# Layer 3 gather loop: offset convolution and indices two blocks ahead, the next image's transform in 17 turns of four per block

## The chip, the cores and the metric

The kernel runs on one core of a Trainium2 chip. The metric is the device time of one execution in microseconds (us). Other times are taken from one profiled execution.

## What is computed

Four layers run one after the other on a batch of four images of 96 channels and 64 x 64 pixels. The change lies in the fourth one (layer 3). For an image it computes, cut to what matters here:

```python
mag  = abs(rfft2(x))                       # -> channel gate ca; with x -> spatial gate sa
y    = x * ca * sa
freq = resize(abs(rfft2(y)).mean(1))
aux  = concat([y, coord, freq])            # 101 channels
offset = conv3x3(aux, off_w)               # 9 taps x 2 coordinates
gate   = sigmoid(conv1x1(relu(conv3x3(aux, dg1_w)), dg2_w))
y_base = conv3x3(y, base_w)
sampled = bilinear(y, xx + offset_x, yy + offset_y)    # 9 taps, 4 corners each
y_def = einsum("bcthw,oct->bohw", sampled, def_w)
z = (1 - gate) * y_base + gate * y_def     # then batch norm, relu, + x
```

## The kernel before

An image's 4096 pixels are cut into 8 blocks (m) of 512, and each block into 4 steps (u) of 128 pixels: 32 blocks and 128 steps in the loop for the four images. The order on every engine is the one in which the program writes it down (a manual schedule), so a waiting instruction holds up all that stands behind it on its engine. The parts of a step and of a block, with their engines:

- gathered(u) (L1970): nine indirect DMAs on GpSimd (L1976), one per tap; each fetches for 128 pixels the four corners of all channels from a table in DRAM. They need the indices ix of the block and a free sm buffer; there are three, so gathered(u) reuses the one that weighted(u-3) read.
- weighted(u) (L1983): ten VectorE operations (L1993 to L1997) multiply sm by the corner weights cw, which lie in PSUM, and add them up into sd.
- transposed(u) (L1999): seven TensorE transposes of sd (L2014), copied by ACT into sT (L2015, L2017).
- mixed(m) (L2019): seven matmuls on sT (yd, L2026); then four VectorE operations beginning with z (L2031), which need yd and write the block's result.
- guides(m) (L1907): the offset and gate convolution (go, nine taps on TensorE, L1899) and two ACT operations (L1912, L1913).
- offsets(m) (L1915): four transposes (of, L1920), then 16 small VectorE operations from L1927 to L1956 that make the indices ix (L1950) and the weights cw of the block.
- bases(m) (L1959): the base convolution (yb, nine taps), a matmul dg, and two ACT operations (L1964, L1968).

While an image is in the loop, the next one is prepared, in chains of four half steps each; every step has two such places, "early" (ahead of weighted) and "late" (behind it):

- attended(b, n), eight per image (L1842): the transfer sab of the spatial gate (L1849, SyncE) and the multiplication of X by both gates (L1851, VectorE); four transposes tp (L1576); the ACT copy xT (L1581) and eight writes of it into the table (L1858, SyncE); four matmuls fa with ACT copies (L1592, L1600).
- columns(b, f0), nine per image (L1864): transposes tf (L1612); an ACT copy fT (L1619); matmuls fb (L1623) and their square on ACT; an addition on VectorE (L1629).
- frequency(b) (L1880): a root on ACT, 33 matmuls fe (L1640) and a copy, one matmul up, and two DMAs that write the frequency channel, which guides of the next image read.

In the loop, gathered(u) is written first, then the early places, then weighted(u-1) and transposed(u-1), then the late ones. Relative to the four steps of block k: mixed(k-1) stands at the second step (matmuls early, z late), guides(k+1) at the second step early, offsets(k+1) at the third (transposes early, VectorE late), bases(k+1) at the fourth early. The chains of attended begin at half steps 1, 5, 9, ... of the 64 of an image, two to a block; columns follow from step 17 on, one each step; frequency takes steps 27 and 28. Before the loop a front (L2047) transforms all images, applies the gates to the first, and makes the first block's guides, offsets and bases.

Of the kernel before, what the change touches and what calls it, by code (L numbers as in the profile page):

```python
# [10 lines left out]
F32 = mybir.dt.float32  # L11
I32 = mybir.dt.int32
# [1783 lines left out]
def layer3(k, X, aux, out):  # L1796

    tc, nc, ins = k.tc, k.nc, k.ins
    with ExitStack() as es:
# [42 lines left out]
        def attended(b, n, tags=None):  # L1842

            table = tables[b % 2]
            s = slice(n * NB, n * NB + NB)
            if n == 0:
                f1[b] = spec.begin()
            sab = wk.tile([C, NB], F32, name="sab")
            nc.sync.dma_start(sab, sa_d[b : b + 1, s].partition_broadcast(C))  # L1849
            y = X[b][:, s]  # L1850
            nc.vector.scalar_tensor_tensor(y, y, ca[:, b : b + 1], sab, ALU.mult, ALU.mult)  # L1851
            yield
            for yT in spec.row_steps(f1[b], 4 * n, y, None, tags):
                if yT is not None:
                    for h2 in range(2):
                        for q in range(4):
                            r, c = 8 * n + h2 + 1 - q // 2, 1 - q % 2
                            nc.sync.dma_start(  # L1858
                                table[r : r + 7 : 2, c : c + W, q].rearrange("r w c -> w r c"),
                                yT[64 * h2 : 64 * h2 + 64],  # L1860
                            )
                yield

        def columns(b, f0, tags=None):  # L1864

            yield from spec.column_steps(f1[b], f0, tags)
# [40 lines left out]
        def guides(m):  # L1907

            p = ps.tile([128, NB], F32, name="go_ps", tag="cv")
            conv(m, p, go_w, 101)  # L1910
            go[m] = wk.tile([82, NB], F32, name="go")
            nc.scalar.activation(go[m][64:82], p[64:82], AF.Identity, bias=go_b[64:82])  # L1912
            nc.scalar.activation(go[m][:50], p[:50], AF.Relu, bias=go_b[:50])  # L1913

        def offsets(m):  # L1915

            n = m % NN
            p = ps.tile([128, NJ, 18], F32, name="of_ps", tag="stp", bufs=1)
            for j in range(NJ):
                nc.tensor.transpose(  # L1920
                    p[:, j], go[m][64:82, 128 * j : 128 * j + 128], k.ident[64:82, 64:82]
                )
            yield
            pt = wk.tile([128, 2, 36], F32, name="pt3")
            pv = p.rearrange("p j (t a) -> p a j t", a=2)
            ptv = pt.rearrange("p a (j t) -> p a j t", t=9)
            nc.vector.tensor_scalar(ptv[:, 0], pv[:, 0], xx, None, ALU.add)  # L1927
            nc.vector.tensor_tensor(
                ptv[:, 1],
                pv[:, 1],  # L1930
                yy[:, 4 * n : 4 * n + 4].unsqueeze(2).to_broadcast([128, 4, 9]),
                ALU.add,
            )

            nc.vector.tensor_scalar(pt, pt, -1.0, float(W), ALU.max, ALU.min)
            it = wk.tile([128, 2, 36], I32, name="it")
            nc.vector.tensor_copy(it, pt)
            fl = wk.tile([128, 2, 36], F32, name="fl")
            nc.vector.tensor_copy(fl, it)
            up1 = wk.tile([128, 2, 36], F32, name="up1")  # L1940
            nc.vector.tensor_tensor(up1, fl, pt, ALU.is_gt)
            nc.vector.tensor_sub(fl, fl, up1)
            nc.vector.tensor_sub(pt, pt, fl)
            at = wk.tile([128, 36], F32, name="at")
            nc.vector.tensor_scalar(
                at, fl[:, 1], float(TW), float(TW + 1), ALU.mult, ALU.add
            )
            nc.vector.tensor_add(at, at, fl[:, 0])
            ix[m] = wk.tile([128, 36], I32, name="ix")
            nc.vector.tensor_copy(ix[m], at)  # L1950

            om = wk.tile([128, 2, 36], F32, name="om")
            nc.vector.tensor_scalar(om, pt, -1.0, 1.0, ALU.mult, ALU.add)  # L1953
            cw[m] = cws[:, m % 2]
            for i, (wy, wx) in enumerate(((om, om), (om, pt), (pt, om), (pt, pt))):
                nc.vector.tensor_mul(cw[m][:, :, i], wx[:, 0], wy[:, 1])  # L1956
            yield
# [78 lines left out]
            nc.vector.bn_stats(stats[:, b, n], z)  # L2036
            yield

        cws = ps.tile([128, 2, 36, 4], F32, name="cws", bufs=1)
        FS = list(range(0, NF, 4))  # L2040

        def once(step):

            step(0)
            yield

        def front(pool):  # L2047

            slots = {}

            def start(at, count, gen):
                for i in range(count):
                    slots.setdefault(at + i, []).append(gen)

            def chains(kind, b, ats):
                for n, at in enumerate(ats):
                    tags = pairs[at % 2]
                    if kind == "rows":
                        start(at, 3, described(b, n, pool, tags))
                    elif kind == "attended":  # L2060
                        start(at, 4, attended(b, n, tags))
                    else:
                        start(at, 4, columns(b, FS[n], tags))

            chains("rows", 0, range(0, 8))
            chains("rows", 1, [8, 9, 10, 12, 14, 16, 18, 20])
            chains("columns", 0, [11, 13, 15, 17, 19, 21, 22, 23, 24])
            chains("columns", 1, range(25, 34))
            start(29, 9, attention(0))
            chains("rows", 2, range(34, 42))  # L2070
            start(39, 9, attention(1))
            chains("attended", 0, range(42, 57, 2))
            chains("columns", 2, [45, 47, 49, 51, 53, 55, 57, 58, 59])
            chains("rows", 3, [43, 61, 63, 65, 67, 69, 71, 73])
            chains("columns", 0, range(60, 77, 2))
            start(63, 9, attention(2))
            chains("columns", 3, range(77, 86))
            start(80, 4, frequency(0))
            start(86, 1, once(guides))
            start(87, 2, offsets(0))  # L2080
            start(89, 1, once(bases))
            start(89, 9, attention(3))
            for t in sorted(slots):
                for step in slots[t]:
                    next(step)
# [4 lines left out]
        def at(where, u, step):  # L2090
            where.setdefault(u, []).append(lambda: next(step))

        def spread(h, n, step):
            for i in range(h, h + n):
                at((early, late)[i % 2], i // 2, step)

        with tc.manual_schedule():
            with tc.tile_pool(name="l3t", bufs=2) as pool:
                front(pool)
            smp = es2.enter_context(tc.tile_pool(name="l3s", bufs=3))  # L2100
            prod = ps.tile([128, 5, 2, C], F32, name="prod", bufs=1)
            for m in range(B * NN):
                u = NJ * (m + 1)
                step = mixed(m)
                at(early, u + 1, step)
                at(late, u + 1, step)
            for m in range(1, B * NN):
                u = NJ * (m - 1)
                early.setdefault(u + 1, []).append(lambda m=m: guides(m))
                step = offsets(m)  # L2110
                at(early, u + 2, step)
                at(late, u + 2, step)
                early.setdefault(u + 3, []).append(lambda m=m: bases(m))
            for b in range(1, B):
                u = NN * NJ * (b - 1)
                for n in range(NN):
                    spread(2 * (u + 2 * n) + 1, 4, attended(b, n))
                u += 2 * NN + 1
                for i, f0 in enumerate(FS):
                    spread(2 * (u + i), 4, columns(b, f0))  # L2120
                spread(2 * (u + len(FS) + 1), 4, frequency(b))
            for u in range(U + 2):
                if u == U - NN * NJ + 1:
                    x0 = spec.begin().rearrange("c f i h -> c (f i h)")[:, :L]
                    nc.sync.dma_start(x0, x_d[0])
                if u < U:
                    gathered(u)
                for step in early.get(u, ()):
                    step()
                if 1 <= u <= U:  # L2130
                    weighted(u - 1)
                    transposed(u - 1)
                for step in late.get(u, ()):
                    step()
# [46 lines left out]
```

## Time and profile before

| what | value |
|---|---|
| median of 21 runs | 8522.75 us (8498.27 to 8545.22) |
| the profiled execution | 8535.59 us; its span 8533.8 us |
| busy share over the span | TensorE 68%, VectorE 68%, ACT 45%, GpSimd 55% |
| loop of layer 3, first gather | 6407.3 us |
| first gathers of blocks 8, 16, 24, 31 | 6917.9, 7448.2, 7962.1, 8409.4 us |
| 6407 to 8409.5 us, busy | TensorE 1156, VectorE 1147, ACT 285, GpSimd 1064 us |
| mean granted TensorE clock | 0.77 |

A line of the page's groups reads: source line, engine, operation, what it writes and reads, shape, count; then the busy time in us and the mean time of one in ns; then the idle time of the engine just before these instructions and what ended most of it. "Remote" means that the profile shows no releaser, "issue" that it shows no wait. A line of a timeline reads: start and duration in us, engine, line, operation, and in brackets the idle time before it with its releaser. The ends of TensorE's matmuls are modelled.

### The profile page before, as it was taken

The page shows a single profiled execution, that of the slowest core. Times are in us where ns is not written, and L with a number is a line of the kernel's source. Part 1 is how long each engine was busy: PE and PEld are TensorE (multiplying, and loading weights), DVE is VectorE, ACT ScalarE, POOL GpSimd, SP SyncE. Part 2 cuts the span into 40 slices and gives each one's busy share as a digit, 9 for nine tenths or more (in the row PEclk, how much of TensorE's full clock was granted, in tenths as well). Part 3 has the DMA queues.
Part 4 walks back from the last instruction along what each step waited for, and adds up shares of the span by engine and source line. Part 5 has one row for each costly group of instructions (what it writes and reads, how often), then busy time and mean ns, then how long its engine had stood idle before and what let it go on. Part 6 is the DMA issues. An engine that isn't in the chain of part 4 may idle for free.

```text
span 8533.8 us, 75977 instructions
## 1 busy us (share of the span) xinstructions
PE 5800.3 (68%) x23706; PEld 2743.9 (32%) x23706; DVE 5837.1 (68%) x8303; ACT 3861.0 (45%) x7432; POOL 4693.3 (55%) x2915
## 2 busy tenths in 40 slices
PE   5667676777677676566697989798755656566553
PEld 1222222222222221422264645455443323333221
DVE  4899899988988989488753635445346556565555
ACT  4666666666666665333254645454431111111111
POOL 4787788777877887144443433324005545455553
PEclk8888878888888787787787878787876777677676
DMA  3222222222222222423210101010015444353333
GB/s 111 95 95 94 94 95 100 97 102 102 94 94 95 94 96 92 150 74 89 70 24 1 39 1 39 1 34 6 23 37 142 124 117 138 100 148 114 113 116 124
DMA packets 424411, 720.27 MB, mean 84 GB/s; under 512 B 188150, under 2 KB 190254, under 8 KB 419763
## 3 DMA queue, kind: packets, MB, share of 16 engines
q1 hardware_dynamic: 348710, 480.74, 18.1%
q0 software_dynamic: 73968, 227.47, 9.2%
q10 hardware_dynamic: 1328, 7.20, 0.2%
q8 instruction: 190, 3.11, 0.1%
q14 instruction: 215, 1.75, 0.1%
HBM read 567.04 MB, written 97.82 MB: 78 GB/s over the span
## 4 chain that ended last, share of the span: by engine, by line
PE 29%; DVE 23%; issue 15%; POOL 14%; another core or an unknown queue 8%; ACT 7%; DMA 2%; SPq 1%; DVEq 0%; POOLq 0%; ACTq 0%
POOL bt L602 7%; DVE bt L593 6%; PE mm_ps L448 6%; DVE bt L566 4%; PE sc_ps L1061 2%; PE pT_ps L1110 2%; POOL sz L526 2%; POOL w L507 2%; PE o_ps L1130 2%; DVE prod L1993 2%; DVE sm L1994 1%; PE yb_ps L1899 1%; ACT a_ps L577 1%; PE m_ps L1510 1%
## 5 line engine op out<-in xcount | busy, mean ns | idle before, releaser
L602 POOL TENSOR_TENSOR bt<-bt,Cb 128x1536 f32<-128x1536 f32 x512 | 1763.6, 3445 | 650.4 <-issue 488.3
L593 DVE TENSOR_TENSOR_SCAN bt<-a_ps,carry,bt 128x512 f32<-128x512 f32 x1536 | 1886.6, 1267 | 58.5 <-ACT a_ps L577 12.3
L1976 POOL DMA_INDIRECT sm<-table,ix x1152 | 1098.2, 953 | 1295.8 <-DVE om L1953 482.3
L577 ACT ACTIVATE a_ps<-dR,w_l_A_log 128x512 f32<-128x512 f32 x1536 | 1052.8, 685 | 535.4 <-DVE bt L593 531.1
L566 DVE TENSOR_TENSOR bt<-xR,Bb 128x1536 f32<-128x1536 f32 x512 | 885.6, 1730 | 219.7 <-issue 198.4
L448 PE MATMUL mm_ps<-h,Wk 96*128 96x512 f32 x1024 | 598.9, 751 | 272.0 <-issue 269.9
L2014 PE MATMUL sT_ps<-ident,sd 128*128 128x128 f32 (+1 forms) x896 | 223.1, 373 | 711.0 <-ACT sT L2015 431.4
L559 PE MATMUL Bb<-dbl,w_c_seln 128*128 128x512 f32 x512 | 366.6, 805 | 335.4 <-DVE bt L566 335.4
L613 PE MATMUL yp<-bt,w_c_red 128*32 128x512 f32 x3072 | 571.2, 658 | 13.2 <-POOL bt L602 13.2
L1098 POOL TENSOR_TENSOR p<-p,rs 128x392 f32<-128x392 f32 x384 | 312.0, 840 | 462.6 <-DVE rs L1096 360.7
L448 PEld LDWEIGHTS mm_ps<-h,Wk 96*128 96x128 f32 x1024 | 240.8, 242 | 636.8 <-issue 629.4
L469 PE MATMUL mm_ps<-xc,w_l_xp 96*128 96x512 f32 x256 | 218.4, 1006 | 289.5 <-POOL xc L463 289.5
L319 PE MATMUL bc_ps<-xs,w_l_bc 96*128 96x512 f32 x384 | 241.7, 762 | 215.3 <-DVE q L906 215.3
L2014 PEld LDWEIGHTS sT_ps<-ident,sd 128*128 128x128 f32 (+1 forms) x896 | 133.0, 181 | 785.0 <-ACT sT L2015 457.7
L1085 ACT ACTIVATE p<-p,rs 128x196 f32<-128x196 f32 x768 | 342.6, 449 | 84.9 <-DVE rs L1075 84.5
L2015 ACT COPY sT<-sT_ps 128x512 f32<-128x512 f32 (+1 forms) x256 | 122.1, 477 | 516.5 <-PE sT_ps L2014 265.1
L1912 ACT ACTIVATE go<-go_ps,w_l_go_b 18x512 f32<-18x512 f32 x32 | 21.7, 678 | 715.6 <-remote 557.2
L2031 DVE SCALAR_TENSOR_TENSOR z<-yd_ps,vec,yb 96x512 f32<-96x512 f32 x32 | 23.9, 747 | 463.9 <-remote 260.1
L1899 PE MATMUL yb_ps<-X,w_l_base_w 96*128 96x504 f32 (+3 forms) x576 | 313.0, 708 | 0.3 <-ACT go L1913 0.3
L1118 DVE COPY pT<-pT_ps 98x512 f32<-98x512 f32 x256 | 176.5, 690 | 172.5 <-PE pT_ps L1110 165.5
L559 PEld LDWEIGHTS Bb<-dbl,w_c_seln 128*128 128x128 f32 x512 | 118.9, 258 | 541.4 <-issue 506.6
L1993 DVE TENSOR_TENSOR prod<-sm,cws 128x960 f32<-128x960 f32 (+1 forms) x256 | 270.8, 1058 | 7.3 <-DVE cws L1956 0.4
(367 smaller groups left out, 12923.9 us busy)
## 6 DMA issues: line engine op xcount, KB each, us to landing
dR<-spread SPq DMA_DIRECT2D x384, 256.0 KB
xR<-spread SPq DMA_DIRECT2D x384, 256.0 KB
Cb<-out_states SPq DMA_DIRECT2D x256, 256.0 KB
spread<-w SPq DMA_DIRECT2D x128, 192.0 KB
spread<-dx SPq DMA_DIRECT2D x128, 192.0 KB
table<-xT SPq DMA_DIRECT2D x256, 96.0 KB
own<-vd SPq DMA_DIRECT2D x512, 36.8 KB
toep<-l_toep SPq DMA_DIRECT2D x12, 1536.0 KB
```

The costliest lines, as they stand in the source:

```text
L448: nc.tensor.matmul(p, Wk[:, i, t, hf], h[:, t : t + T], start=t == 0, stop=t == 3)
L559: nc.tensor.matmul(Bb, seln[:, nq], st["dbl"], start=True, stop=True)
L566: nc.vector.tensor_mul(bt, st["xR", hf], Bb.unsqueeze(1).to_broadcast([128, NG, T]))
L577: nc.scalar.activation(dec[n], st["dR", hf][:, q], AF.Exp, scale=A[:, i, nq, hf, q : q + 1])
L593: nc.vector.tensor_tensor_scan(t, dec.pop(n), t, carry_of(v)[:, q : q + 1], ALU.mult, ALU.add)
L602: nc.gpsimd.tensor_mul(bt, bt, st["Cb"][nq].unsqueeze(1).to_broadcast([128, NG, T]))
L613: nc.tensor.matmul(st["yp", hf][32 * q : 32 * q + 32], red, bt[:, q], start=nq == 0, stop=nq == NQ - 1,)
L1085: nc.scalar.activation(ps[n][:, h, i], ps[n][:, h, i], AF.Exp, scale=-1.0, bias=rs[n][:, 0, h, i : i + 1], accum_out=rs[n][:, 1, h, i : i ...
L1899: nc.tensor.matmul(dv[:, r0:r1, c0:c1], w_[:, t], av[b][:ch, 8 * n + r0 + dy : 8 * n + r1 + dy, c0 + dx : c1 + dx], start=t == 4, stop=t == 8,
L1976: nc.gpsimd.indirect_dma_start(sm[u][:, t].rearrange("p q c -> p (q c)"), None, samples[m // NN % 2], bass.IndirectOffsetOnAxis(ap=ix[m][: ...
L1993: nc.vector.tensor_mul(p, v[:, :, 2:4], w_[:, :, 2:4])
L2014: nc.tensor.transpose(p[: e - 128 * q, q - q0], sf[:, 128 * q : e], k.ident)
```

## The change

The offset convolution and the index arithmetic of a block are moved one block earlier: while block k is in the loop, guides(k+2) and offsets(k+2) stand where guides(k+1) and offsets(k+1) stood; bases stays. For this ix has three buffers instead of two and cws three slots instead of two, and the front makes the guides and offsets of block 1 as well. The chains of the next image's transform begin at other places: in each block of eight half steps there are four turns, at 0, 2, 5 and 7; eight chains of attended begin one half step ahead of turns 1 to 8, nine of columns at turns 10 to 18, and frequency four half steps behind the last.

```diff
-            ix[m] = wk.tile([128, 36], I32, name="ix")
+            ix[m] = wk.tile([128, 36], I32, name="ix", bufs=3)
...
-            cw[m] = cws[:, m % 2]
+            cw[m] = cws[:, m % 3]
...
-        cws = ps.tile([128, 2, 36, 4], F32, name="cws", bufs=1)
+        cws = ps.tile([128, 3, 36, 4], F32, name="cws", bufs=1)
...
-            start(86, 1, once(guides))
+            start(86, 1, once(guides, 0))
             start(87, 2, offsets(0))
-            start(89, 1, once(bases))
+            start(89, 1, once(bases, 0))
+            start(90, 1, once(guides, 1))
+            start(91, 2, offsets(1))
             start(89, 9, attention(3))
...
             for m in range(1, B * NN):
                 u = NJ * (m - 1)
-                early.setdefault(u + 1, []).append(lambda m=m: guides(m))
-                step = offsets(m)
-                at(early, u + 2, step)
-                at(late, u + 2, step)
+                if m + 1 < B * NN:
+                    early.setdefault(u + 1, []).append(lambda m=m + 1: guides(m))
+                    step = offsets(m + 1)
+                    at(early, u + 2, step)
+                    at(late, u + 2, step)
                 early.setdefault(u + 3, []).append(lambda m=m: bases(m))
             for b in range(1, B):
-                u = NN * NJ * (b - 1)
+                h = 2 * NN * NJ * (b - 1)
+                turns = [h + 2 * NJ * k + x for k in range(5) for x in (0, 2, 5, 7)]
                 for n in range(NN):
-                    spread(2 * (u + 2 * n) + 1, 4, attended(b, n))
-                u += 2 * NN + 1
-                for i, f0 in enumerate(FS):
-                    spread(2 * (u + i), 4, columns(b, f0))
-                spread(2 * (u + len(FS) + 1), 4, frequency(b))
+                    spread(turns[n + 1] - 1, 4, attended(b, n))
+                for f0, turn in zip(FS, turns[NN + 2 :]):
+                    spread(turn, 4, columns(b, f0))
+                spread(turn + 4, 4, frequency(b))
```

More of the change, by code (lines that the diff above doesn't have):

```diff
@@ L2037, in mixed, with once @@
             yield
-        cws = ps.tile([128, 2, 36, 4], F32, name="cws", bufs=1)
+        cws = ps.tile([128, 3, 36, 4], F32, name="cws", bufs=1)
         FS = list(range(0, NF, 4))
-        def once(step):
-            step(0)
+        def once(step, m):
+            step(m)
             yield
```

## The prediction

> **What bounds the kernel now.** I read the page first, then the order of the instructions on each engine in both programs, then the timeline of single blocks. Only the layer 3 loop changes: it runs from the first gather at 6407.3 us to the end of the last block at about 8500 us, of a span of 8533.8 us. The first gathers of blocks 0, 8, 16, 24 and 31 start at 6407.3, 6917.9, 7448.2, 7962.1 and 8409.4 us: 510.6, 530.3 and 513.9 us for eight blocks each with a transform of the next image in them, 447.3 us for seven blocks without one (63.9 each). From the page's groups:
>
> ```profile
> L1976 POOL DMA_INDIRECT sm<-table,ix x1152 | 1098.2, 953 | 1295.8 <-DVE om L1953 482.3
> L1912 ACT ACTIVATE go<-go_ps,w_l_go_b 18x512 f32<-18x512 f32 x32 | 21.7, 678 | 715.6 <-remote 557.2
> L2031 DVE SCALAR_TENSOR_TENSOR z<-yd_ps,vec,yb 96x512 f32<-96x512 f32 x32 | 23.9, 747 | 463.9 <-remote 260.1
> ```
>
> GpSimd waits 482.3 us for the indices: this is the wait that the change attacks. But VectorE waits 463.9 us at z, with no releaser named. One plain block, timelines of GpSimd, TensorE and VectorE (start, duration, what; idle before):
>
> ```profile
> 8133.77 0.95 POOL L1976 DMA_INDIRECT sm<-table,ix  x1 [0.30 <-issue]
> 8153.76 0.95 POOL L1976 DMA_INDIRECT sm<-table,ix  x1 [19.04 <-DVE om L1953]
> ```
>
> ```profile
> 8108.53 8.15 PE L2026 MATMUL yd_ps<-sT,w_l_def_w 128*128 128x512 f32 x14
> 8116.52 7.81 PE L1899 MATMUL go_ps<-X,w_l_go_w 101*128 101x512 f32 x18
> 8124.17 0.60 PE L2014 MATMUL sT_ps<-ident,sd 128*128 128x128 f32 x4
> ```
>
> ```profile
> 8114.10 0.55 DVE L1997 TENSOR_TENSOR sd<-sm,prod 128x384 f32<-128x384 f32 x1
> 8140.38 0.75 DVE L2031 SCALAR_TENSOR_TENSOR z<-yd_ps,vec,yb 96x512 f32<-96x512 f32 x1 [25.73 <-remote]
> ```
>
> z needs yd, which by the trace ends at 8116.7; z starts 23.7 us later, at 8140.38, which is 5.7 us after the last gather of the run was issued (8134.7). In blocks 23 to 30 this distance is 5.7 us each time. Over the loop, TensorE's results reach ACT or VectorE over 1 us late only when gathers were running (all 18 late z, all 20 late go). A run of gathers up to some 14 us old shows no lateness, one over 19 us old mostly does, and a pause of GpSimd ends it about 5 us after the last issue. So the chain of a plain block is: 36 gathers (44.8 us), 5.7 us, z (2.9), W (8.0), the indices (2.6), next gather: 64 us. (W(u) is the ten VectorE operations of weighted(u).)
>
> In blocks with the transform a second wait stands in VectorE's queue, at the multiplication of attended (L1851). Timelines of SyncE, ACT and VectorE:
>
> ```profile
> 7584.21 5.25 SPq L1858 DMA_DIRECT2D table<-xT  x8
> 7589.57 0.72 SPq L1849 DMA_DIRECT2D sab<-sa_d  x1
> ```
>
> ```profile
> 7583.70 0.49 ACT L1581 COPY xT<-tp_ps 128x384 f32<-128x384 f32 x1
> ```
>
> ```profile
> 7594.83 0.75 DVE L1851 SCALAR_TENSOR_TENSOR X<-X,ca,sab 96x512 f32<-96x512 f32 x1 [5.25 <-DMA sab<-sa_d]
> ```
>
> The sab transfer is queued on SyncE behind the eight table writes of the turn before, which wait for that turn's xT. From the start of xT to the next multiplication: 11.1 us.
>
> **The change, part by part.** Nothing is removed; the third ix and cws buffers cost no instruction.
>
> *Indices a block earlier.* VectorE's order keeps its places (z, W, indices, W, W, W); only the indices are those of a block later. The gather's wait on them goes. What is late next is its buffer: three sm buffers, so gather(u) waits for W(u-3), and the first gather of a block for the W that follows z. That W ended 2.6 us before the old start. TensorE's lateness remains, because GpSimd pauses no earlier. The second gather step waits for the W behind the indices: 3.5 + 8.0 = 11.5 us against 11.26 us for nine gathers (1.2517 each), +0.3. New plain block: 44.8 + 0.3 + 5.7 + 2.9 + 8.0 = 61.6 us, gain 2.3. Over the last image 7 x -2.3 = **-16**.
>
> Here a rule of the Trainium skill speaks against my reading: *SBUF — State Buffer*, section "Who interferes with whom", says that DMA never contends with a compute engine and that PE and ACT wait on no one. By it z would follow yd, and the block would be GpSimd's 45.1 us: 31 x (64.6 - 45.1) = 604 us saved, an estimate (64.6 is the mean of the 31 blocks to 8409.4). The rows above (23.7 us late, only beside gathers) disagree, and I go by them.
>
> *Front.* guides(1) and offsets(1) come before the loop. go (7.5 us, row at 6376.91) stands ahead of fe, which waited until 6399.52 for ACT; TensorE was free from 6394.5, so fe starts at 6402.0: +2.5, and of 0.4 ahead of up. The first gather waits for this chain (ACT maps): **+3**. The 3.5 us of indices on VectorE lie before W(0), which gathers need only 34 us later: nothing, as the first gathers cover it.
>
> *Seventeen turns.* Before, an image's eight attended turns lay two to a block over four blocks, the nine columns one to a step after them, the frequency map in the last steps. Now attended takes four places a block, over two blocks and the edge of a third. Same instructions, same DMAs (64 table writes, 8 sab); SyncE's order becomes sab, tables, sab, tables, sab, sab, tables, tables: of each four multiplications one has its sab ahead of the tables, three wait for tables of a turn just before. VectorE's order puts each in front of a different W: a stall there now delays the W that frees a gather's buffer. With E the end of a run of gathers, t the end of the W after z:
>
> - First block: z at E+5.7. ACT then does go twice, the sT copies, xT (go at 7165.30 to xT at 7168.57: 3.3 us): xT at E+9.1, multiplication at E+20.2, 0.75, W 8.0: next block's first gather at E+29. Block 45.1 + 29 = 74.1.
> - Second: xT stands on ACT behind yb, which follows TensorE's convolution: 11.6 us after t (8151.2 to 8162.8), then g: xT at t+13.4, multiplication t+24.5, W to t+33.2. The next has its sab: W to t+42. The third's tables wait for xT behind sT copies (2.2) and two fa (3.0): t+47.2, multiplication t+58.3, W to t+67.1. z, then xT at t+69.3, multiplication t+80.4, W to **t+89.2**.
> - Third: as before to t+33.2, W to t+42 and t+50; its gathers then run from t+33.2 to t+67. yd falls at about t+52, 19 us into that run. Prompt gives 67, late 67 + 5.7 + 2.9 + 8 = 83.6. The plain block's first lateness is at 18.8 us, so I take 83.6.
>
> - Columns fill two blocks. Their adds (L1629) now follow sT by some 3.5 us instead of standing behind a convolution (idle 6.5, 14.9, 0.9, 6.6 in block 20). Without late signals 55 us, with them 65.5; the nearest rows, old column blocks, are 60.6 to 63.3. I take 60 each.
> - Frequency: fe stands in the late stretch, beside z's own wait; when that cover is gone, it costs its 7 to 10 us. 64.
> - Two plain blocks, 61.6 each. Here something is won: the last three blocks of an image took 208, 215 and 214 us, because the frequency map came at the edge (ACT's copy of fe idle before it 37 us, z 39 us), now three blocks before.
>
> Per image 74.1 + 89.2 + 83.6 + 120 + 64 + 123.2 = 554.1, against 510.6, 530.3, 513.9: +43.5, +23.8, +40.2. **Sum**: 43.5 + 23.8 + 40.2 + 3 - 16 = **+94.5 us**. Against the profiled execution's 8535.6 us (span 8533.8) that is 8630; that one ran 12.9 us over the median of 21 runs, 8522.75, so I forecast 8522.75 + 94.5 = **8617 us**.
>
> **Rivals.**
> 1. *The crowded transform stays hidden.* If xT and sab are always out before VectorE comes to the multiplication (its idle there at most 5.6 us as now), each block is as a plain one, 61.6: 492.8 an image, -17.8 - 37.5 - 21.1 - 16 + 3 = -89, **8433**. For it: SyncE is nearly idle, and a multiplication waits for no work of its own block. Against: tables and sab are one in-order queue, and 11.1 us is longer than the 8.0 of one W. It decides at 31.5 us an image: if the three crowded blocks together take under 215 us (72 each, not 82), the kernel is not slower.
> 2. *Crowding is about paid* by the edge and by column blocks at 55: 3 x (2 x 5) and third blocks at 75 give 8617 - 30 - 26 = 8561, with shorter stalls 8500 to 8560.
> 3. *Longer runs of gathers.* Without the index wait GpSimd may run through five steps; then go is late and the indices hold VectorE: 45.1 + 5 + 2.5 + 3.5 + 8 = 64 a plain block, 65.5 a column block, no gain anywhere: +16 + 3 x (5 + 11) = 64 more, **8680**. For it: go is late at 25 us of a run in every block.
> That the change does nothing is excluded: the orders show the indices a block earlier and all turns moved.
>
> **How the numbers follow.** Forecast 0.60 (+40 to +150), rival 1 0.17, rival 2 0.18 (half of it within 0.2%, 0.02 faster, 0.07 slower), rival 3 0.05. 0.2% (17 us) is about what a measurement of this kernel can tell from no change. Faster 0.19, same 0.09, slower 0.72. The range reaches into rival 1, to 8465, and to 8690 for rival 3 and late signals in columns; about 0.2 is left out. The likeliest case alone: 8563 to 8673.
>
> **What would show it.** GpSimd's idle before L1976 named "DVE om" goes, and "DVE sd" or "DVE sm" (W) takes its place; VectorE's idle before L1851 grows from 119 us in the loop to over 200; blocks 1, 9 and 17 take over 80 us; plain blocks about 61.6; the last two blocks of each image lose their 10 to 15 us. I am wrong if the crowded blocks take under 72 us, or if plain blocks fall to 50 because the lateness goes.

## The result

The changed kernel is slower: 8683.1 us median (8668.3 to 8704.8, 8 runs) against 8522.7 us (8490.2 to 8553.7, 56 runs), a ratio of 1.0192 with a 95% interval of 1.0177 to 1.0207. That is +160 us where +94.5 was forecast, and 66 us above the predicted 8617: inside the whole range (8465 to 8690), 10 us above the +40 to +150 of the forecast case.

The profiled execution took 8642.6 us, 40 us under the median of its kernel (that of the kernel before was 13 us over its own). From the page of the changed kernel:

```profile
span 8640.9 us, 75992 instructions
...
L1976 POOL DMA_INDIRECT sm<-table,ix x1152 | 1099.1, 954 | 1393.2 <-DVE sd L1997 432.2
...
L1912 ACT ACTIVATE go<-go_ps,w_l_go_b 18x512 f32<-18x512 f32 x32 | 21.7, 678 | 730.9 <-remote 586.5
```

GpSimd's wait named "DVE om" (the indices) is gone. In its place stand 432 us for sd, the end of a W, which frees the buffer of a gather, and 264 us under the name "DVE pt L1928". These too are waits for the buffer, as the edge behind plain block 15 shows on VectorE and GpSimd. The gather starts 0.3 us after the end of W and before the indices behind that W are written.

```profile
7490.92 0.55 DVE L1997 TENSOR_TENSOR sd<-sm,prod 128x384 f32<-128x384 f32 x1
...
7493.61 0.33 DVE L1950 CAST ix<-at 128x36 int32<-128x36 f32 x1
```

```profile
7491.74 0.94 POOL L1976 DMA_INDIRECT sm<-table,ix  x1 [16.69 <-DVE pt L1928]
```

VectorE's groups over the whole span, two lines of the kernel before first, then three of the changed one:

```profile
L1851 DVE SCALAR_TENSOR_TENSOR X<-X,ca,sab 96x512 f32<-96x512 f32 x32 | 23.9, 747 | 180.1 <-DMA sab<-sa_d 148.2 <-issue 32.0
...
L1927 DVE TENSOR_SCALAR pt<-of_ps,w_c_xx 128x36 f32<-128x36 f32 x32 | 8.0, 251 | 95.3 <-PE of_ps L1920 95.3
```

```profile
L2031 DVE SCALAR_TENSOR_TENSOR z<-yd_ps,vec,yb 96x512 f32<-96x512 f32 x32 | 23.8, 745 | 327.8 <-remote 253.6 <-PE yd_ps L2026 74.1
...
L1851 DVE SCALAR_TENSOR_TENSOR X<-X,ca,sab 96x512 f32<-96x512 f32 x32 | 23.9, 746 | 317.1 <-DMA sab<-sa_d 295.3 <-issue 21.7
...
L1927 DVE TENSOR_SCALAR pt<-of_ps,w_c_xx 128x36 f32<-128x36 f32 x32 | 8.0, 250 | 217.8 <-PE of_ps L1920 217.8
```

VectorE waits less at z (464 us before; the share named "remote" hardly falls, from 260.1 to 253.6, and what falls is the wait for yd itself, from 157.9 to 74.1), more at the multiplication of attended (317 against 180; in the loop alone 255.9 against 119.0), and more at the indices (218 against 95). The last was not in the forecast.

Where the +107 us between the two profiled executions lie, from the first gather of each block:

| stretch | before, us | after, us | difference | forecast |
|---|---|---|---|---|
| up to the first gather | 6407.3 | 6395.1 | -12.2 | +3 |
| image 0 | 510.6 | 547.8 | +37.2 | +43.5 |
| image 1 | 530.3 | 548.8 | +18.5 | +23.8 |
| image 2 | 513.9 | 547.4 | +33.5 | +40.2 |
| image 3, seven blocks | 447.3 | 459.7 | +12.4 | -16 |
| from the last block's first gather | 124.4 | 142.1 | +17.7 | 0 |

The first three blocks of an image (forecast 74.1, 89.2, 83.6) took 72.2, 86.8, 81.7, then 72.0, 88.1, 82.1, then 72.1, 88.3, 81.9 us. Here is why the second is the longest: SyncE, VectorE and GpSimd in block 17 of the changed kernel (timelines: start, duration, what, idle before).

```profile
7578.51 5.25 SPq L1858 DMA_DIRECT2D table<-xT  x8
7583.86 1.02 SPq L1849 DMA_DIRECT2D sab<-sa_d  x2
```

```profile
7587.18 0.75 DVE L1851 SCALAR_TENSOR_TENSOR X<-X,ca,sab 96x512 f32<-96x512 f32 x1 [20.13 <-DMA sab<-sa_d]
```

```profile
7573.86 0.95 POOL L1976 DMA_INDIRECT sm<-table,ix  x1 [0.31 <-issue]
7596.03 1.21 POOL L1976 DMA_INDIRECT sm<-table,ix  x1 [21.22 <-DVE sd L1997]
```

The sab transfer is issued when the eight table writes ahead of it are out of SyncE's queue. VectorE stands 20 us at the multiplication with W behind it, and the gathers stand 21 us behind that W. (In this execution the multiplications that waited came 9.0 to 11.7 us after the xT before them, where the prediction had 11.1.)

From block 22 to 30 the loop is in another state: 65.2 to 68.7 us a block in place of 60 to 62. GpSimd, TensorE and ACT in the last image:

```profile
8115.11 0.95 POOL L1976 DMA_INDIRECT sm<-table,ix  x1 [0.30 <-issue]
8136.51 0.95 POOL L1976 DMA_INDIRECT sm<-table,ix  x1 [20.44 <-DVE sd L1997]
```

```profile
8087.77 7.81 PE L1899 MATMUL go_ps<-X,w_l_go_w 101*128 101x512 f32 x18
```

```profile
8121.42 0.68 ACT L1912 ACTIVATE go<-go_ps,w_l_go_b 18x512 f32<-18x512 f32 x1 [40.11 <-remote]
```

And VectorE there:

```profile
8124.80 0.25 DVE L1927 TENSOR_SCALAR pt<-of_ps,w_c_xx 128x36 f32<-128x36 f32 x1 [24.82 <-PE of_ps L1920]
```

The gathers no longer stop at the edge of a block. A run is still four steps long (36 gathers), but it goes from the second step of a block through the edge to the end of the first step of the next; the last run has seven steps. go, complete at 8095.6 by the trace, reaches ACT at 8121.42, 5.4 us after the run has ended. The indices stand in VectorE's queue ahead of the next W and hold it for 24.8 us. This is the wait of the prediction's rival 3, with runs of four steps where it had spoken of five, in nine of 31 blocks.

### The profile page after: what moved, and what is told of

Its sections match the earlier page's. It is cut to its first block, busy times and chain, and to the rows that moved or that the text cites. A ratio compares the mean times of both kernels' runs of the same rounds, so it can differ in the third digit from the quotient of the medians.

```text
span 8640.9 us, 75992 instructions
## 1 busy us (share of the span) xinstructions
PE 5769.1 (67%) x23706; PEld 2725.7 (32%) x23706; DVE 5839.6 (68%) x8303; ACT 3860.7 (45%) x7432; POOL 4694.5 (54%) x2915
## 4 chain that ended last, share of the span: by engine, by line
PE 29%; DVE 23%; POOL 15%; issue 14%; another core or an unknown queue 8%; ACT 7%; DMA 2%; SPq 1%; DVEq 0%; POOLq 0%; ACTq 0%
POOL bt L602 7%; DVE bt L593 6%; PE mm_ps L448 5%; DVE bt L566 4%; PE sc_ps L1061 2%; PE yb_ps L1899 2%; PE pT_ps L1110 2%; POOL sz L526 2%; DVE prod L1993 2%; POOL w L507 2%; DVE sm L1994 2%; PE o_ps L1130 2%; ACT a_ps L577 1%; DVE prod L1995 1%
## 5 line engine op out<-in xcount | busy, mean ns | idle before, releaser
L1085 ACT ACTIVATE p<-p,rs 128x196 f32<-128x196 f32 x768 | 342.6, 449 | 84.0 <-DVE rs L1075 83.6
L559 PEld LDWEIGHTS Bb<-dbl,w_c_seln 128*128 128x128 f32 x512 | 119.0, 258 | 541.2 <-issue 506.1
L1994 DVE TENSOR_TENSOR sm<-sm,cws 128x960 f32<-128x960 f32 (+1 forms) x256 | 267.8, 1046 | 0.0
```

The costliest lines, as they stand in the source:

```text
L559: nc.tensor.matmul(Bb, seln[:, nq], st["dbl"], start=True, stop=True)
L1994: nc.vector.tensor_mul(v[:, :, 0:2], v[:, :, 0:2], w_[:, :, 0:2])
```

## The experiments

Theory 1: the crowding of attended (sab behind the table writes) is the loss. Theory 2: the indices two blocks ahead cost by themselves, through longer runs of gathers. The runs were on four chips (numbers 7, 3, 1 and 15), on all of which the kernel before takes 7942 to 7947 us, not 8523. The chip of the first runs is not named in their records, and may be one of these at another time; I call it the first chip. Each kernel below is compared with the kernel before on its own chip. The kernel before has a profile on chip 3 alone, so sums that set another chip's profile beside it go across chips. The times in us that the first expectations name were meant for the first chip; on the others the ratios are what can be compared, against 1.0192 there.

**The turns alone.** The 17 turns of the diff on the kernel before; guides, offsets, ix and cws untouched.

> The kernel before with the 17 turns alone; guides and offsets stay one block ahead, ix and cws keep two buffers. Theory 1 (crowding): the three crowded blocks still take 72, 88 and 82 us, and the indices ahead had gained 2.3 us in each plain block, so this kernel is as slow as the changed one or slower, 8680 us or more. Theory 2 (the longer runs of gathers cost): without the indices ahead GpSimd pauses at each block's edge, no block is in the state of 65.7 us, plain blocks are at 64 again, and the kernel takes 8600 to 8640 us.

Measured: 8178.7 against 7944.7 us, 1.0291 (1.0262 to 1.0319), chip 7. The stall at L1851 in the loop is 260.3 us, and the crowded blocks take 48 to 56, 87 to 90 and 64 to 66 us: without the indices ahead the loss is all there, as theory 1 had it.

**Sab one chain ahead**, in the changed kernel:

```diff
-            sab = wk.tile([C, NB], F32, name="sab")
-            nc.sync.dma_start(sab, sa_d[b : b + 1, s].partition_broadcast(C))
+            for i in range(n + 1 if n else 0, min(n + 2, NN)):
+                sabs[b, i] = wk.tile([C, NB], F32, name="sab")
+                nc.sync.dma_start(
+                    sabs[b, i],
+                    sa_d[b : b + 1, i * NB : i * NB + NB].partition_broadcast(C),
+                )
...
```

> The changed kernel with each sab transfer issued one chain earlier, ahead of the table writes that stood before it. Theory 1 (the multiplication of attended waits for sab behind the tables): VectorE's idle time before L1851 falls from 256 us to under 60, the crowded blocks fall from 72, 88, 82 to 62 to 72 each, and the time falls by 70 to 130 us, to 8555 to 8615. Theory 2 (longer runs of gathers): the idle time moves to z and to the indices, the time falls by less than 30 us.

Measured: 7980.4 us, 1.0043 (1.0029 to 1.0057), chip 7: 198 us less than the turns alone on the same chip. The stall at L1851 in the loop is 96.8 us, where under 60 was expected, and all of it is named for sab: at the places where the chains stand closest, a sab issued one chain earlier still stands behind table writes.

**Pauses of GpSimd**, in the changed kernel:

```diff
+        hold = wp.tile([128, 128], F32, name="hold")
...
+                    if u % 2 == 0:
+                        for i in range(10):
+                            nc.gpsimd.memset(hold, 0.0)
                     gathered(u)
```

> The changed kernel with ten small writes on GpSimd (about 2.1 us, no DMA) before every second step of gathers. If TensorE's results are late only because gathers run for more than some 19 us without a pause, each run is now 23 us at most, VectorE's idle time at z (272 us) and at the indices (218 us) falls under 100 us each, plain blocks fall from 61.6 or 65.7 to 50 to 54 us, and the time falls to 8400 to 8520. If the lateness has nothing to do with the length of a run, the pauses add up to 16 x 4 x 2.1 = 134 us at most and gain nothing: 8683 to 8815.

Measured: 8251.1 us, 1.0388 (1.0359 to 1.0416), chip 7. Every plain block took 50.6 to 51.6 us. What this run was to test was not there: in the other three profiles of this chip, without any pause, no z is over 0.1 us late. So the pauses only added time, and neither expectation was tested.

**Looser turns**, indices two blocks ahead:

```diff
                 for n in range(NN):
...
+                    spread(h + 3 * n + 1, 4, attended(b, n))
+                for i, f0 in enumerate(FS):
+                    spread(h + 27 + 2 * i, 4, columns(b, f0))
+                spread(h + 46, 4, frequency(b))
```

> The changed kernel, indices two blocks ahead, with the attended chains three half steps apart (2.7 a block, not 4), columns two half steps apart behind them and the frequency map just ahead of the guides that read it. Theory 1 (crowding): with more distance between the table writes and the next sab the idle time before L1851 falls to some 120 to 180 us, and the time to 8540 to 8620. Theory 2 (longer runs of gathers): the distance does not matter, and the time stays at 8640 or more.

Measured: 8185.4 us, 1.0304 (1.0275 to 1.0333), chip 7. A miss for theory 1 as I had put it: VectorE's idle time at L1851 in the loop is 265.6 us, no less than in the changed kernel. The table writes of a chain are its third half step. With chains four half steps apart, as in the kernel before, the next sab comes two half steps behind them; with three, one. By this run one is too few. My reading is that the distance from the table writes to the next sab in SyncE's queue counts, not the number of turns in a block; two spacings do not prove it.

**The changed kernel and the kernel before, again**, chip 3:

> The changed kernel itself once more, since the second chip takes 7945 us where the first took 8523 us for the kernel before. If the chip is again one on which z is not late, plain blocks take 45 to 46 us, the crowded ones 60 to 90, and the time is 8170 to 8240 against some 7945 (turns alone: 8179): then the whole loss is the crowding, and it is larger than on the first chip since the plain blocks no longer hide it. If z is late, it is 1.0177 to 1.0207 of the kernel before, as at first.

> The kernel before once more, for a profile on this chip. If TensorE's results are late only on the first chip, VectorE's idle time at z falls from 464 us to under 100 and plain blocks from 64 to 45 to 50 us; the blocks of each image's end, where the frequency map was late, stay at 60 to 70. If the lateness is in every chip, the blocks are as in the first profile, 64 us.

Measured: 8169.6 against 7943.8 us, 1.0271 (1.0237 to 1.0304). Blocks without a transform take 45.0 to 45.4 us in the changed kernel's last image, and the crowded ones 49 to 56, 88 and 66 to 67. One part of the second expectation was missed: the blocks of each image's end in the kernel before did not stay at 60 to 70 us but took 45 to 52. Three lines of the groups in the loop's window, the kernel before first:

```profile
L1976 POOL DMA_INDIRECT sm<-table,ix x1152 | 1098.2, 953 | 741.5 <-ACT maps L1652 347.2 <-issue 330.8 <-DVE om L1953 33.2
L2031 DVE SCALAR_TENSOR_TENSOR z<-yd_ps,vec,yb 96x512 f32<-96x512 f32 x32 | 23.8, 744 | 45.6 <-PE yd_ps L2026 45.6
L1851 DVE SCALAR_TENSOR_TENSOR X<-X,ca,sab 96x512 f32<-96x512 f32 x24 | 17.9, 747 | 94.6 <-DMA sab<-sa_d 94.6
```

The changed kernel, the same window:

```profile
L1976 POOL DMA_INDIRECT sm<-table,ix x1152 | 1099.4, 954 | 971.7 <-ACT maps L1652 349.6 <-issue 323.4 <-DVE sd L1997 204.6
L2031 DVE SCALAR_TENSOR_TENSOR z<-yd_ps,vec,yb 96x512 f32<-96x512 f32 x32 | 23.8, 744 | 45.7 <-PE yd_ps L2026 45.7
L1851 DVE SCALAR_TENSOR_TENSOR X<-X,ca,sab 96x512 f32<-96x512 f32 x24 | 17.9, 745 | 259.0 <-DMA sab<-sa_d 259.0
```

z waits the same 46 us in both, for its own yd, never for "remote". GpSimd had waited 482 us for the indices on the first chip and waits 33 us here, so there was next to nothing for the change to remove ("ACT maps" is the wait ahead of the first gather, "issue" the 0.3 us between gathers). The stall at sab is about that of the first chip (259 us, 256 there), and here the gathers pay for most of it: from the first gather of block 0 to that of block 31 the changed kernel takes 1676.4 us, the kernel before 1447.3, and 1401 would be nothing but gathers at 45.2 a block. A plain block of the kernel before on chip 3, GpSimd, TensorE and VectorE:

```profile
7724.47 7.81 PE L1899 MATMUL go_ps<-X,w_l_go_w 101*128 101x512 f32 x18
```

```profile
7722.68 0.95 POOL L1976 DMA_INDIRECT sm<-table,ix  x1 [0.30 <-issue]
7723.93 0.95 POOL L1976 DMA_INDIRECT sm<-table,ix  x1 [0.30 <-issue]
7725.18 0.95 POOL L1976 DMA_INDIRECT sm<-table,ix  x1 [0.30 <-issue]
```

```profile
7725.43 0.74 DVE L2031 SCALAR_TENSOR_TENSOR z<-yd_ps,vec,yb 96x512 f32<-96x512 f32 x1
```

TensorE passes from yd to go at 7724.5, and z follows at 7725.4 with no idle time, in the middle of a run of gathers that has gone on since 7482 us without a pause. On the first chip the same step took 23.7 us.

**The indices alone**, on the kernel before. Its transform ends too late for the guides of the next image's first block, so that one keeps its place:

```diff
+                ahead = [i for i in (m, m + 1) if i % NN == 0 or i == m + 1]
+                ahead = [i for i in ahead if i < B * NN and (i % NN or i == m)]
+                for x, i in enumerate(ahead):
+                    early.setdefault(u + 1 + x, []).append(lambda i=i: guides(i))
...
```

> The kernel before with the indices two blocks ahead alone: the transform keeps its old places, so the first block of an image, whose guides need the frequency map, keeps its indices one block ahead, and the block ahead of it makes two sets. Theory 2 (indices ahead cost by themselves): 0.5% slower or more. Theory 1: where z is prompt the gathers wait for indices only in the last three blocks of an image (some 6 us each), so 0 to 30 us are gained, at most 0.4%; where z is late, up to 2.3 us a block, 0.2 to 0.6% faster.

Measured: 7938.1 against 7946.8 us, 0.9995 (0.9980 to 1.0009), chip 1. Nothing that can be told from noise, either way.

**Looser turns and sab ahead**, both edits above in the changed kernel:

> The changed kernel with attended chains three half steps apart, as in the run before, and each sab issued one chain ahead. If the whole loss is that the multiplication waits for sab behind the table writes (theory 1), both remedies together leave nothing of it: within 0.3% of the kernel before, and, since the edge of an image is then free, up to 0.4% faster. If table writes or VectorE's own work are the limit, it stays where sab ahead alone was, at 1.004, or above.

Measured: 7921.9 us, 0.9970 (0.9956 to 0.9984), chip 1. This is within what theory 1 had expected. But the gain is not the loop's: it takes 1467.9 us, 20.6 more than that of the kernel before on chip 3 (blocks 4, 5, 12, 13, 20, 21, in which the columns stand close, take 47 to 59). The front gives it: from the first multiplication of attended to the first gather 158.6 us, where the kernel before has 199.6.

**Sab ahead on the kernel before**, nothing else:

> The kernel before with nothing changed but each sab issued one chain ahead, in the front and in the loop. Theory 1 (sab behind the table writes): the front's attended chains lose their wait too, as the first gather came 45 us earlier in the two earlier runs with sab ahead; the loop, in which the old spacing already hides most of it, gains 0 to 10 us. So 45 to 55 us less: 0.9930 to 0.9945 of the kernel before. If the front's gain came from something else in the changed kernel, 0.999 to 1.000.

**The same with a handshake** that ends a run of gathers until a result of TensorE has reached ACT:

```diff
+        seen = wp.tile([1, 1], F32, name="seen")
...
+                    if u % NJ == 3 and u + 1 < U:
+                        nc.gpsimd.tensor_copy(seen, go[u // NJ + 1][:1, :1])
                     gathered(u)
```

> The same, and GpSimd copies one number of go (the next block's guide) before the fourth step of gathers in each block, so that a run of gathers stops until TensorE's result has reached ACT. On a chip on which z is late: the pause of some 5.7 us takes the place of the wait at the block's edge of 5.7 + 2.9 + 8.0 us, blocks fall from 64 to 51 to 54 us, and the time falls by 250 to 400 us. On a chip on which it is prompt: go is there some 24 us into a block and is asked for at 34, so the copies cost some 31 x 0.2 us and a little in the blocks with the transform: 0 to 30 us more than the run before.

Measured, both on chip 15: 7859.9 us, **0.9887** (0.9869 to 0.9904), and 7870.9 us, 0.9908 (0.9895 to 0.9922), against 7943.5. The first has the lowest ratio of all kernels tried and is faster than both of this case. The gain is 84 us where 45 to 55 were expected: the front gives 36.9 (199.6 to 162.7), and the loop gives 42.7 (1447.3 to 1404.6), where I had put 0 to 10. Its lines, in the loop's window (the line numbers are 4 and 6 higher):

```profile
L1982 POOL DMA_INDIRECT sm<-table,ix x1152 | 1098.4, 953 | 663.5 <-issue 329.3 <-ACT maps L1652 312.5 <-DVE prod L2001 11.7
L1855 DVE SCALAR_TENSOR_TENSOR X<-X,ca,sab 96x512 f32<-96x512 f32 x24 | 17.9, 744 | 5.4 <-DMA sab<-sa_d 5.4
```

The stall at sab falls from 94.6 us in the kernel before to 5.4, and GpSimd waits for nobody any more: its 1152 gathers are one run, with some 0.3 us between any two (the 11.7 us at "DVE prod" are 37 such gaps), 45.0 to 46.0 us a block. The old spacing had not hidden the 95 us. As I read it, VectorE fell behind in the blocks with attended, and the gathers paid in the fifth to seventh block of each image, 46.1 to 52.4 us on chip 3, 45.2 to 45.6 here. The kernel with the handshake took 11 us more, though the intervals overlap, and had no lateness to remove.

**The handshake alone, and the turns with sab ahead**, chip 1:

> The kernel before with the handshake alone: GpSimd copies one number of go before the fourth step of gathers of each block. Where z is late: blocks fall from 64 to 51 to 54 us, 250 to 400 us less. Where z is prompt: its ratio to the kernel before is 1.000 to 1.004, as the handshake cost 0.2% beside sab ahead.

> The kernel before with the 17 turns and sab one chain ahead, indices one block ahead as in the kernel before. The changed kernel with sab ahead took 1.0043 of the kernel before. If what is left of the loss there is VectorE's own work in the crowded blocks, this one takes the same, 1.003 to 1.007. If the indices ahead made part of it, this one takes 0.997 to 1.002. Where z is late, theory 1 has it at 0.99 to 1.005 against 1.019 for the changed kernel.

Measured: 7956.9 us, 1.0018 (1.0004 to 1.0031), and 7980.3 us, 1.0048 (1.0030 to 1.0066), against 7942.0. Both as expected for a chip on which z is prompt.

## Why the prediction came out as it did

**How near the number came.** Part of it is luck. In the profiled executions (+107 us against +94.5) images 0 to 2 took 89.2 us more where 107.5 were forecast, the last image with its end 30.1 more where 16 less were forecast, and the part up to the first gather 12.2 less where 3 more were forecast: the errors cancel. The median's +160 us lies 3 us from rival 3's 8680, though the one execution with a trace was in rival 3's state for nine blocks only.

**The crowding** (theory 1) is shown to be the loss on the four chips. Sab ahead brings the changed kernel from 1.0271 (chip 3) to 1.0043 (chip 7), 2.3% or some 180 us; by the two profiles, which lie 191 us apart, 46 come from the front (202.0 to 155.9) and 150 from the loop (1676.4 to 1526.7), with the stall at L1851 down from 259 to 97 us. The loop's other 79 us above the kernel before stay with sab ahead, whether the indices are one block ahead (1.0048) or two (1.0043): they belong to the turns, where the profile still names sab for 97 us; whether that is all of it was not tried. On the first chip, where only the two kernels were run, the traces show the same blocks carrying it: nine crowded blocks within 2.5 us of the forecast, 725 us where 741 were forecast and 552 stood before; the other 15 blocks of these images won back 84. That the loss on the first chip would go with sab ahead was not tried.

**The indices** cost nothing and gain nothing where z is prompt: the turns alone took 1.0291, with the indices 1.0271; the indices alone 0.9995. Theory 2 falls for those chips.

**Steps that held on the first chip.** The wait named "DVE om" went and sd took its place. The stall at L1851 grew to 255.9 us in the loop (forecast: over 200). Plain and column blocks of images 0 and 1 took 60.2 to 61.9 us (forecast 61.6 and 60; the block of the frequency map, forecast 64, took 60.2 and 61.1). The last three blocks of an image, 208 to 215 us before, took 182 to 184.

**Steps that failed.**
- *"Over the last image 7 x -2.3 = -16"*: measured +12.4, and +17.7 behind it. The blocks of some 61.6 us held only to block 20. Block 21 took 47.6 us, its last run of gathers went through the edge, and from then on the loop was in the state of rival 3, which I had given 0.05, at some 65.7 us a block. So forecast and rival were not two cases but two states of one loop: the run of gathers is ended either behind z (61.6) or behind the indices (65.7). That a run which passes an edge unstopped is what changes the state is read from this one passage. The step that missed this is "GpSimd pauses no earlier": without the index wait nothing ensures that it pauses there at all. At the end, z of block 30 waited 45.4 us for its yd in a run that went on to the last gather: ACT had waited 37.3 us for the result of bases, with the copies that yd needs behind it. The sum had no such term.
- *Front +3*: from the first multiplication of attended to the first gather the first chip shows 199.5 before and 199.2 after, chip 3 199.6 and 202.0. At most 2.4 us; the layers ahead differ by more from run to run.
- *Rival 1* needed the three crowded blocks under 215 us; they took 241 to 242. *Rival 2* had the third block at 75; it took 82. On chip 3 it took 66 and the column blocks 52 to 55, so rival 2's mechanism is seen where z is prompt, but there the kernel before is also faster and the loss is larger, not smaller.
- *"VectorE waits 463.9 us at z, with no releaser named"*: only 260.1 us of these have none; 157.9 are named for yd itself.

**What stays open.** The medians of the first chip differ by 160 us, the profiled executions by 107. If other executions pass into the slower state earlier, 13 more blocks at 4.1 us would make the 53 us; only profiled executions have traces, so this is argued, not shown. And I did not learn why the results of TensorE were late there, nor whether that belongs to the chip or to the time of those runs: no experiment was on it. By the traces the gathers run at the same pace (0.95 us and 0.30 between them) on all chips. My reading, that a run of over 19 us makes them late, is not a law of the program: the same program on chip 3 runs gathers for hundreds of us, and in the twelve profiles of the four chips no z and no go is over 0.5 us late. A slower TensorE alone does not explain it: the loop's TensorE busy time is 1156 us on the first chip and 1107 on chip 3, 49 us apart where the loops are 555 apart, and in the plain block shown in the prediction TensorE had begun the transposes behind go at 8124.17, 16 us before z. Whether pauses or the handshake shorten the block of 64 us could not be tried, since no chip of the experiments showed the lateness.

The Trainium skill, *SBUF — State Buffer*, section "Who interferes with whom", which I had weighed against my rows, says that DMA never contends with a compute engine and that PE and ACT wait on no one. The estimate drawn from it was a block of 45.1 us and 604 us less. In the last image, whose blocks have no transform, they take 45.0 to 45.7 us in eleven of the twelve profiles of the four chips (the run with the pauses left out), and the kernel before is 579 us faster than on the first chip; there the page describes what is seen. On the first chip the block does not come out so: 18 of 32 z were late, by up to 24 us, only beside gathers. Whether the gathers' DMA is what made them late is not shown.

## What to carry to other kernels

A small load that an engine waits for should not be issued behind writes that wait for another engine's results: issue it one turn earlier, which cost no instruction here and was worth 1.1% in the kernel before and 2.3% in the changed one, on the chips where it was tried. Before work is crowded into fewer places, count in the in-order queue what will stand between a producer's writes and the next consumer's load; the same transform at twice the rate turned 95 us of stall into 259. And a wait that is removed may have been what kept a pipeline in step: ask what will stop the engine next, and whether it stops it in the same place each time.

## What the runs showed of the hardware

- One program, 7% apart: 8523 us in the runs on the first chip, 7942 to 7947 in those on chips 7, 3, 1 and 15. The traces of the first and of chip 3 are 10 us apart up to the first gather (6407.3 and 6397.6 us); the other 580 us lie behind it, 555 of them up to the first gather of block 31, in the loop of indirect gathers, where only on the first chip TensorE's results reach ACT and VectorE up to 26 us late while gathers are running. The mean granted clock of the two profiles is 0.770 and 0.793.
- A loop with two states in one execution of one program: 60 to 62 us a block, five blocks in a row, and, behind one block of 47.6 us, 65 to 69 us for nine blocks to the end.
- Ten writes of 128x128 on GpSimd before every second step of gathers lengthened a block that the gathers fill, and that has two such pauses, by 5.4 to 5.8 us (seven blocks of the last image: 356.3 us, against 315.8 to 318.8 in the eleven other profiles of the four chips).
